# Forming delta*u*B of a selective scan on TensorE with a diagonal that GpSimd selects

## The chip, the cores and the metric

The kernel runs on one core of a Trainium2 chip. The metric is the device time of one execution in microseconds (us), lower is better. The engines of the core are TensorE (PE in the profile; the loading of its weights is PEld), VectorE (DVE), ScalarE (ACT), GpSimd (POOL) and SyncE (SP), which issues the DMAs. SBUF is the on-chip memory of 128 partitions, PSUM the memory that TensorE writes its results to.

## The reference

The model has four layers on 4 images of 64 x 64 pixels with 96 channels. Layers 0 and 1 are selective scans over the image in four directions; layers 2 and 3 are attention and a small network on tokens. The change touches only the scans. For each image, direction k and channel d (192 channels) the reference computes, over L = 4096 positions and 16 states n:

```
delta = softplus(dt_proj(dts) + bias)
dA = exp(delta * A[d, n])
h = dA * h + (delta * u) * B[n]        # one recurrence per channel and state
y = sum over n of h * C[n]             # B and C are projections of u, shared by all channels
result = y + D[d] * u                  # D is then summed over the four directions
```

B and C depend on position, state, direction and image, but not on the channel. The results of the four directions are added up.

## The kernel before, in words

Two images are scanned together, and there are two such pairs and two scan layers: four scans, each a `PairScan`. Partitions hold channels. An image has 192 channels, so a scan has three tiles of partitions: j = 0 holds 128 channels of the first image, j = 1 the same 128 of the second ("own" tiles), and j = 2 the remaining 64 channels of both (the "shared" tile). The sequence is cut into chunks of T = 1024 positions. A step is one (direction k, chunk ci, tile j), 4 x 4 x 3 = 48 steps a scan, 192 in all. A step goes through 16 states in 8 groups of NG = 2.

For each state DVE runs one hardware scan along the 1024 positions, `h = da * h + bp` (line 715). Its two inputs are da = exp(delta*A), from ScalarE, and delta*u*B. The latter is made in one of three ways, and a letter for each state in the strings OWN and SHARED (line 45) says which; `maker` looks it up:

- V: TensorE spreads the row of B over the partitions by a product with a selection matrix, `sel` (line 592), into the PSUM tile bp, and DVE multiplies it in place by du = delta*u (line 712).
- A: ScalarE scales the transposed du (`dut`, positions on partitions) by B, which is then a scalar per partition (`outer`, line 541; the tile x), and TensorE transposes the eight 128x128 blocks into bp (line 588).
- G: a DMA spreads the row of B over the partitions (tile bb, line 562), GpSimd multiplies it by du (tile dbu, line 575), and ScalarE writes the exponential into bp (line 585).

B in the transposed form is the tile bt, with positions on partitions, 8 blocks, and 32 columns (16 states of each image); it is the last entry of `projected`, and `dut` the last of `made`.

After the scan GpSimd copies the last value of each row for the next chunk (tile last, line 728) and multiplies h in place by C, which a DMA has spread over the partitions (tile cb, line 730). TensorE sums the 16 states: it transposes each h into the PSUM tile yp, where the passes accumulate (`onto_time`, line 617). The first term of yp is D*u in direction 0 (ScalarE scales u into the tile skip, line 636, and eight transposes add it), and in the other directions the sum so far, read back from memory (tile kept). ScalarE copies yp out (ysum, line 663).

All engines follow the program's order (`InOrder`), so the order of the main loop (line 680) is the order of each engine's queue. In the turn of group g it issues: the loads of bb for group g+2; the bp products of group g; the sum of group g-3 (LAG = 3; h has four buffers); what is made ahead for group g+1 (x, da, cb, dbu); the V products and the scans of group g; pieces of the next step's delta and du and of the next chunk's projection at fixed places (`drive`); and last, on GpSimd, the copy of last and the two C products of group g. bp has two buffers of PSUM, x has two, da four, cb three, dbu and bb one.

Every instruction inside the scans passes through the helper at line 71, so the profile puts them all on L71, and they are told apart by their tiles.

Of the kernel before, what the change touches and what calls it, by code (L numbers as in the profile page):

```python
# [16 lines left out]
F32 = mybir.dt.float32  # L17
BF16 = mybir.dt.bfloat16
# [3 lines left out]
ALU = mybir.AluOpType  # L22
# [4 lines left out]
HW = 64  # L27
# [4 lines left out]
D1 = DI - D0  # L32
NS = 16
R = 6
K = 4
NP = 32 * 3
# [3 lines left out]
T = 1024  # L40
NG = 2
LAG = 3


OWN, SHARED = "VAVAVAAGVAVAVAVA", "VGVAVAVGVAVGVAVV"
NT = L // 128
HID = 4 * C
EPS = 1e-5
# [7 lines left out]
class InOrder:  # L56


    def __init__(self, tc):
        for name in ("tensor", "vector", "scalar", "gpsimd"):  # L60
            setattr(self, name, InOrderEngine(tc, getattr(tc.nc, name)))
        self.sync = tc.nc.sync
# [22 lines left out]
class ScanLayer:  # L85


    def __init__(self, tc, pw, dram, x_src, w, n):
        nc = tc.nc

        self.last = n == 1
        self.x_src, self.w = x_src, w
        self.x_dst = dram.tile([NB * L, C] if self.last else [NB, C, L], F32, name=f"x{n + 1}")

        self.norms = [[], []]

        self.zg = [dram.tile([3, 128, L], F32, name=f"zg{n}{pr}") for pr in range(NB // 2)]
        self.y = [dram.tile([2, L, DI], F32, name=f"y{n}{pr}") for pr in range(NB // 2)]
        self.par = par = pw.tile([128, 2, P_ALL], F32, name=f"par{n}")
        nc.sync.dma_start(out=par, in_=w["par"].rearrange("s p c -> p s c"))  # L100

        self.amat = pw.tile([128, 2, K * NS], F32, name=f"amat{n}")
        nc.scalar.activation(self.amat, par[:, :, P_A : P_A + K * NS], AF.Exp)
        nc.vector.tensor_scalar(self.amat, self.amat, -1.0, None, ALU.mult)
        self.dsum = pw.tile([128, 2, 1], F32, name=f"dsum{n}")
        nc.vector.tensor_reduce(self.dsum, par[:, :, P_D : P_D + K], mybir.AxisListType.X, ALU.add)


class GroupNorm:
# [260 lines left out]
class PairScan:  # L370
# [5 lines left out]
    def __init__(self, tc, pk, pq, pd, cst, ident, u, layer, pr):  # L376
        self.tc, self.pk, self.pq, self.pd = tc, pk, pq, pd
        self.cst, self.ident, self.u = cst, ident, u
        self.par, self.amat, self.dsum = layer.par, layer.amat, layer.dsum
        self.w, self.y = layer.w, layer.y[pr]  # L380
        self.weights = {0: load_weights(tc.nc, pk, self.w, 0)}
        self.projected, self.made = [], []
# [103 lines left out]

    def scan(self, stage, nc):
        tc, ident, steps, projected, made = self.tc, self.ident, self.steps, self.projected, self.made
        amat, dsum, w, y, weights, chunk_of = self.amat, self.dsum, self.w, self.y, self.weights, self.chunk_of
        sel = self.cst["sel"]  # L490
        pk = self.pk
        p2 = stage.enter_context(tc.tile_pool(name="b_2", bufs=2))
# [20 lines left out]
                pieces[0] = next(pieces[1])  # L513

        groups = [(at, n) for at in range(len(steps)) for n in range(0, NS, NG)]
        of = (0, 128, 64)

        def maker(g, i):
            at, n0 = groups[g]
            return (SHARED if steps[at][2] == 2 else OWN)[n0 + i]  # L520
# [37 lines left out]
            return cb  # L558

        bbs = {}  # L560

        def start_bb(g):

            at, n0 = groups[g]
            for i in range(NG):
                if maker(g, i) == "G":
                    bbs[g, i] = p2.tile([128, 1, T], F32, name="bb", bufs=1)
                    spread(bbs[g, i], projected[at // 3][2], steps[at][2], 2 * NS + n0 + i)

        def start_dbu(g):  # L570
            out = {}
            for i in range(NG):
                if (g, i) in bbs:
                    out[i] = p2.tile([128, T], F32, name="dbu", bufs=1)
                    nc.gpsimd.tensor_tensor(out[i], made[groups[g][0]][1], bbs.pop((g, i))[:, 0], ALU.mult)
            return out

        def start_bp(g, i, xs):


            at, n0 = groups[g]
            _, _, j = steps[at]
            bp = pm.tile([128, T], F32, name="bp", bufs=2)
            if maker(g, i) == "G":
                exp_of(bp, g, i)
            elif maker(g, i) == "A":
                for t in range(T // 128):
                    nc.tensor.transpose(bp[:, 128 * t : 128 * t + 128], xs[i][:, t], ident)
            else:
                for hf in range(2):  # L590
                    cols = slice(512 * hf, 512 * hf + 512)
                    nc.tensor.matmul(
                        bp[:, cols],
                        sel[:, n0 + i, of[j] : of[j] + 128],
                        projected[at // 3][1][:, cols],
                        start=True,
                        stop=True,
                    )
            return bp
# [3 lines left out]
        def add_up(g, i, h):  # L603

            at, n0 = groups[g]
            n = n0 + i
            if n == 0:
                sums[at] = yp = pm.tile([128, T // 128, 128], F32, name="yp")
                if at in skips:
                    onto_time(yp, skips.pop(at), True, False)  # L610
                else:
                    before = kept.pop(at)
                    for t in range(0, T // 128, 4):
                        nc.tensor.matmul(yp[:, t : t + 4], ident, before[:, t : t + 4], start=True, stop=False)
            onto_time(sums[at], h[:, i], False, n == NS - 1)

        def onto_time(yp, v, first, final):

            for t in range(T // 128):
                nc.tensor.matmul(  # L620
                    yp[:, t],
                    v[:, 128 * t : 128 * t + 128],
                    ident,
                    start=first and t % 4 == 0,
                    stop=final and t % 4 == 3,
                    is_transpose=True,
                )

        skips = {}

        def start_skip(at):

            k, _, j = steps[at]
            if k == 0:
                skips[at] = p2.tile([128, T], F32, name="skip", bufs=1)
                nc.scalar.mul(
                    skips[at].rearrange("p (a b) -> p a b", b=HW), projected[at // 3][0][j], dsum[:, j // 2]
                )

        def places(at, tile_):  # L640
# [25 lines left out]

        for g in range(2):
            start_bb(g)
        ahead, cb_next, dbu_next = start_ahead(0), start_cb(0), start_dbu(0)
        hs = {}  # L670

        def sum_of(g):
# [7 lines left out]
        for g, (at, n0) in enumerate(groups):  # L680
# [9 lines left out]
                discretising = begun(begin_discretise(at + 1)) if at + 1 < len(steps) else []  # L690
            if n0 == 8 and at + 1 < len(steps):
                load_kept(at + 1)
            (da, xs), cb, dbu = ahead, cb_next, dbu_next
            if g + 2 < len(groups):
                start_bb(g + 2)

            bps = [start_bp(g, i, xs) for i in range(NG)]
            if g >= LAG:
                sum_of(g - LAG)
            if n0 == 0:  # L700
                start_skip(at)
            if n0 == NS - NG:
                drive(discretising, n0)
                drive(projecting, (j, n0))
            if g + 1 < len(groups):
                ahead, cb_next, dbu_next = start_ahead(g + 1), start_cb(g + 1), start_dbu(g + 1)

            hs[g] = h = p2.tile([128, NG, T], F32, name="h", bufs=LAG + 1)
            du = made[at][1]
# [230 lines left out]
def hybrid_kernel(ctx: ExitStack, tc: tile.TileContext, a):  # L940
# [14 lines left out]
    with ExitStack() as scans:  # L955
        pw = scans.enter_context(tc.tile_pool(name="s_w", bufs=1))
        pn = scans.enter_context(tc.tile_pool(name="s_n", bufs=1))
        units = []
        for n in range(2):
            layer = ScanLayer(tc, pw, dram, x, {k: a[f"l{n}_{k}"] for k in ("par", "wi", "wx", "wdt", "wo")}, n)  # L960
            units += [(layer, pr) for pr in range(NB // 2)]
            x = layer.x_dst
        units[0][0].after = units[2][0]
        with ExitStack() as scanning:
            pk = scanning.enter_context(tc.tile_pool(name="s_k", bufs=2))
            pu = scanning.enter_context(tc.tile_pool(name="s_u", bufs=1))
            pq = scanning.enter_context(tc.tile_pool(name="s_q", bufs=1))
            pd = scanning.enter_context(tc.tile_pool(name="s_d", bufs=2, space=DRAM))
            cst["sel"] = pu.tile([NP, NS, 256], BF16, name="sel")
            nc.sync.dma_start(out=cst["sel"], in_=a["c_sel"])  # L970
            cst["ident16"] = pu.tile([128, 128], BF16, name="ident16")
            nc.vector.tensor_copy(cst["ident16"], ident)
            u = [pu.tile([128, L], F32, name=f"u{j}") for j in range(3)]
            before = None
            for unit in units:
                scan = PairScan(tc, pk, pq, pd, cst, ident, u, *unit)
                between_scans(tc, cst, ident, half, pn, u, before, scan, unit)
                scan.run()
                before = unit
        token_layers(tc, cst, ident, half, x, before, a)  # L980


def constants():
# [2 lines left out]
    import numpy as np  # L986


    sel = np.zeros((3, 2, NS, NS, 2, 128), ml_dtypes.bfloat16)
    for n in range(NS):  # L990
        for i in range(2):
            sel[:, i, n, n, i] = 1
# [1 line left out]
    group = np.where(at[:, None] // 3 == at[None] // 3, np.float32(1) / np.float32(3), np.float32(0))  # L994
    heads = np.where(at[:, None] // 16 == at[None] // 16, np.float32(0.25), np.float32(0))
    return {
        "c_sel": sel.reshape(NP, NS, 256),
        "c_group": group.astype(np.float32),
        "c_heads": heads.astype(np.float32),
    }  # L1000
# [93 lines left out]
```

## Time and profile before

The profile page gives the profiled execution's own time only as its span.

| | |
|---|---|
| median of 3 runs | 10596.84 us (10596.55 to 10597.79) |
| span of the profiled execution | 10592.1 us |
| DVE busy | 9610.8 us (91%) |
| GpSimd busy | 9023.9 us (85%) |
| ScalarE busy | 8761.4 us (83%) |
| TensorE busy, weight loads | 8027.2 us (76%), 5946.6 us (56%) |
| mean granted TensorE clock | 0.885 |
| moved by DMA | 2120.41 MB, mean 200 GB/s |

How to read a row of the groups: line, engine, operation, output<-inputs, shape, xcount; then the busy time of the group in us and the mean duration of one instruction in ns; then the idle time of the engine just before these instructions, and what ended most of it. Busy time counts overlapping instructions once, so busy time divided by the count can be less than the mean. The two longest groups are GpSimd's product of h with C (3072 instructions, 7196.5 us) and DVE's scans (3072 in four groups).

### The profile page before, as it was taken

What the parts mean: (1) busy time and instruction counts of PE and PEld (TensorE: products, weight loads), DVE (VectorE), ACT (ScalarE), POOL (GpSimd) and SP (SyncE); (2) the same over time, 40 slices, a digit from 0 to 9 for tenths busy, and PEclk for the clock granted to TensorE, in tenths of its full rate; (3) what the DMA queues carried; (4) which work ended last, traced back from release to release, by engine and by line L of the source; (5) the groups of instructions that cost most, each with busy time, mean ns of one, the idle gap of its engine ahead of it and who ended that gap; (6) DMA issues with size and microseconds to landing.
All of it is one profiled execution on the core that took longest, in us unless ns stands there. A gap on an engine that the chain in (4) does not pass through costs nothing. (4 is left out here: it accounts for less than half of the span.)

```text
span 10592.1 us, 142441 instructions
## 1 busy us (share of the span) xinstructions
PE 8027.2 (76%) x47648; PEld 5946.6 (56%) x47648; DVE 9610.8 (91%) x6922; ACT 8761.4 (83%) x18779; POOL 9023.9 (85%) x5298
## 2 busy tenths in 40 slices
PE   7777777777777777777877777777877777777666
PEld 4555555554555555555555555555555565555554
DVE  8999999998999999998899999999799999999755
ACT  6888888885988888887788888888688888888666
POOL 3999999993999999997599999999399999999645
PEclk9888898989888898998888988898888989899877
DMA  5677777776677777777567777777667777777710
GB/s 155 208 212 216 220 220 218 219 218 164 205 212 212 218 220 218 217 220 210 158 206 213 219 220 220 223 213 216 162 207 212 216 213 225 221 217 213 195 32 25
DMA packets 905174, 2120.41 MB, mean 200 GB/s; under 512 B 330582, under 2 KB 640152, under 8 KB 706712
## 3 DMA queue, kind: packets, MB, share of 16 engines
q1 hardware_dynamic: 904440, 2111.30, 69.5%
q8 instruction: 378, 6.19, 0.3%
q14 instruction: 356, 2.92, 0.1%
HBM read 1949.56 MB, written 161.48 MB: 199 GB/s over the span
## 5 line engine op out<-in xcount | busy, mean ns | idle before, releaser
L71 POOL TENSOR_TENSOR h<-h,cb 128x1024 f32<-128x1024 f32 x3072 | 7196.5, 2367 | 226.4 <-issue 62.6
L71 DVE TENSOR_TENSOR_SCAN h<-da,last,bp 128x1024 f32<-128x1024 f32 x2064 | 4736.6, 2335 | 146.7 <-PE bp L71 22.8
L71 ACT ACTIVATE x<-dut,bt 128x128 f32<-128x128 f32 x12288 | 3495.9, 371 | 1.4 <-PE bp L71 1.1
L71 PE MATMUL yp<-ident,h 128*128 128x128 f32 x24576 | 3359.4, 297 | 10.5 <-POOL h L71 10.5
L71 PEld LDWEIGHTS yp<-ident,h 128*128 128x128 f32 x24576 | 3188.5, 157 | 126.6 <-issue 76.6
L71 ACT ACTIVATE da<-delta,amat 128x1024 f32<-128x1024 f32 x2752 | 3062.3, 1139 | 96.6 <-DVE h L71 95.8
L71 PE MATMUL bp<-ident,x 128*128 128x128 f32 x10240 | 1678.5, 316 | 1294.1 <-DVE h L71 956.8
L71 PEld LDWEIGHTS bp<-ident,x 128*128 128x128 f32 x10240 | 1361.3, 163 | 1854.8 <-ACT x L71 1017.4
L71 DVE TENSOR_TENSOR bp<-du,bp 128x1024 f32<-128x1024 f32 x1472 | 1780.5, 1214 | 259.8 <-PE bp L71 257.8
L71 DVE TENSOR_TENSOR_SCAN h<-da,bp 128x1024 f32<-128x1024 f32 x688 | 1537.7, 2275 | 49.9 <-ACT da L71 9.6
L71 PE MATMUL bp<-bparts,sel 96*128 96x512 bf16 x2944 | 920.5, 398 | 756.3 <-DVE h L71 740.4
L71 PEld LDWEIGHTS <-sel 96*128 96x128 bf16 x2944 | 226.8, 100 | 1550.2 <-DVE h L71 1037.8
L71 ACT ACTIVATE bp<-delta,amat 128x1024 f32<-128x1024 f32 x320 | 358.1, 1119 | 526.3 <-DVE h L71 524.6
L71 POOL TENSOR_TENSOR dbu<-du,bb 128x1024 f32<-128x1024 f32 x320 | 755.7, 2362 | 0.0
L71 DVE TENSOR_TENSOR_SCAN h<-bp,last,dbu 128x1024 f32<-128x1024 f32 x240 | 558.9, 2329 | 16.9 <-POOL dbu L71 15.9
L71 PE MATMUL xps<-u,wx 128*76 128x512 f32 x720 | 532.2, 824 | 0.0
L71 POOL COPY last<-h 128x2 f32<-128x2 f32 x1152 | 217.7, 189 | 357.2 <-DVE h L71 355.5
L81 POOL TENSOR_TENSOR ln_rs<-ln_ve,half 128x4 f32<-128x4 f32 x64 | 89.8, 1403 | 483.1 <-DVE ln_ve L79 405.9
L71 ACT ACT_TABLE_LOAD x380 | 487.5, 1283 | 15.9 <-PE bp L71 9.2
L71 POOL TENSOR_TENSOR du<-delta,u 128x1024 f32<-128x1024 f32 x188 | 496.8, 2642 | 0.0
L71 PE MATMUL dps<-cdt,wdt 12*128 12x512 f32 x752 | 433.6, 656 | 0.0
L71 ACT COPY ysum<-yp 128x1024 f32<-128x1024 f32 x192 | 194.5, 1013 | 287.1 <-PE yp L71 287.1
(159 smaller groups left out, 6312.6 us busy)
## 6 DMA issues: line engine op xcount, KB each, us to landing
cb<-crow SPq DMA_DIRECT2D x1024, 1024.0 KB
cb<-crow SPq DMA_DIRECT2D x1024, 512.0 KB
bb<-crow SPq DMA_DIRECT2D x384, 256.0 KB
bb<-crow SPq DMA_DIRECT2D x128, 512.0 KB
y<-ysum SPq DMA_DIRECT2D x192, 256.0 KB
kept<-y SPq DMA_DIRECT2D x160, 256.0 KB
y<-ysum SPq DMA_DIRECT2D x64, 512.0 KB
zt<-zg SPq DMA_DIRECT2D x64, 384.0 KB
```

Of the source, the lines that this page charges most:

```text
L71: return self.tc.keep_in_program_order(getattr(self.engine, op)(*args, **kwargs))
L81: nc.gpsimd.tensor_tensor(rs, ve, half, ALU.pow)
```

## The change

Part of the states of the own tiles are made in a fourth way, D. GpSimd forms, for each of the eight blocks of 128 positions, a 128x128 matrix with B of this state on its diagonal and zero elsewhere: an affine_select over the broadcast column of bt, 128x1024 elements in all (tile dg, one buffer). TensorE multiplies the transposed du block by it, which gives delta*u*B with channels on partitions, in bp. The OWN string goes from VAVAVAAGVAVAVAVA (7 V, 8 A, 1 G) to VDAAVDAAVDAAVAVA (5 V, 8 A, 3 D); SHARED stays. The selects for group g+1 are issued after the dbu products of group g+1, in the turn of group g.

D*u is added by TensorE: a diagonal matrix of D (tile skip of the layer, made once) is multiplied with u as the weights, into yp, in place of ScalarE's scaling and eight transposes.

The selection matrix has 128 columns a state in place of 256. For the shared tile they are used as they are; for an own tile one column is broadcast to 128 with a step of zero.

```diff
-OWN, SHARED = "VAVAVAAGVAVAVAVA", "VGVAVAVGVAVGVAVV"
+OWN, SHARED = "VDAAVDAAVDAAVAVA", "VGVAVAVGVAVGVAVV"
...
+        self.skip = pw.tile([128, 2, 128], F32, name=f"skip{n}")
+        for s in range(2):
+            nc.vector.tensor_scalar(self.skip[:, s], ident, self.dsum[:, s], None, ALU.mult)
...
-        of = (0, 128, 64)
...
+        zero = self.tc.nc.gpsimd.to_reg(0.0)
...
+        def start_diagonals(g):
+
+            at, n0 = groups[g]
+            j = steps[at][2]
+            out = {}
+            for i in range(NG):
+                if maker(g, i) == "D":
+                    out[i] = p2.tile([128, T // 128, 128], F32, name="dg", bufs=1)
+                    col = NS * j + n0 + i
+                    nc.gpsimd.affine_select(
+                        out=out[i],
+                        in_=projected[at // 3][4][:, :, col : col + 1].to_broadcast([128, T // 128, 128]),
+                        compare_op=ALU.is_equal,
+                        fill=zero,
+                        base=0,
+                        pattern=[[0, T // 128], [-1, 128]],
+                        channel_multiplier=1,
+                    )
+            return out
...
+            elif maker(g, i) == "D":
+                for t in range(T // 128):
+                    nc.tensor.matmul(
+                        bp[:, 128 * t : 128 * t + 128], made[at][2][:, t], dgs[i][:, t], start=True, stop=True
+                    )
             else:
+                if j == 2:
+                    chosen = sel[:, n0 + i]
+                else:
+                    chosen = sel[:, n0 + i, D1 * j : D1 * j + 1].to_broadcast([NP, 128])
                 for hf in range(2):
                     cols = slice(512 * hf, 512 * hf + 512)
                     nc.tensor.matmul(
                         bp[:, cols],
-                        sel[:, n0 + i, of[j] : of[j] + 128],
+                        chosen,
                         projected[at // 3][1][:, cols],
                         start=True,
                         stop=True,
...
-                if at in skips:
-                    onto_time(yp, skips.pop(at), True, False)
+                k, ci, j = steps[at]
+                if k == 0:
+                    for t in range(T // 128):
+                        there = T * ci + 128 * t
+                        nc.tensor.matmul(
+                            yp[:, t],
+                            self.u[j][:, there : there + 128],
+                            self.skip[:, j // 2],
+                            start=t % 4 == 0,
+                            stop=False,
+                        )
                 else:
...
-        def start_skip(at):
-
-            k, _, j = steps[at]
-            if k == 0:
-                skips[at] = p2.tile([128, T], F32, name="skip", bufs=1)
-                nc.scalar.mul(
-                    skips[at].rearrange("p (a b) -> p a b", b=HW), projected[at // 3][0][j], dsum[:, j // 2]
-                )
...
-            bps = [start_bp(g, i, xs) for i in range(NG)]
+            bps = [start_bp(g, i, xs, dgs) for i in range(NG)]
             if g >= LAG:
                 sum_of(g - LAG)
-            if n0 == 0:
-                start_skip(at)
...
             if g + 1 < len(groups):
                 ahead, cb_next, dbu_next = start_ahead(g + 1), start_cb(g + 1), start_dbu(g + 1)
+                dgs_next = start_diagonals(g + 1)
...
-            cst["sel"] = pu.tile([NP, NS, 256], BF16, name="sel")
+            cst["sel"] = pu.tile([NP, NS, 128], BF16, name="sel")
```

More of the change, by code (lines that the diff above doesn't have):

```diff
@@ L85, with __init__ @@
 class ScanLayer:
-    def __init__(self, tc, pw, dram, x_src, w, n):
+    def __init__(self, tc, pw, dram, ident, x_src, w, n):
         nc = tc.nc
@@ L378, in __init__ @@
         self.cst, self.ident, self.u = cst, ident, u
-        self.par, self.amat, self.dsum = layer.par, layer.amat, layer.dsum
+        self.par, self.amat, self.skip = layer.par, layer.amat, layer.skip
         self.w, self.y = layer.w, layer.y[pr]
@@ L488, in scan @@
         tc, ident, steps, projected, made = self.tc, self.ident, self.steps, self.projected, self.made
-        amat, dsum, w, y, weights, chunk_of = self.amat, self.dsum, self.w, self.y, self.weights, self.chunk_of
+        amat, w, y, weights, chunk_of = self.amat, self.w, self.y, self.weights, self.chunk_of
         sel = self.cst["sel"]
@@ L576, in start_dbu, with start_bp @@
             return out
-        def start_bp(g, i, xs):
+        def start_bp(g, i, xs, dgs):
             at, n0 = groups[g]
@@ L614, in add_up, with onto_time @@
                         nc.tensor.matmul(yp[:, t : t + 4], ident, before[:, t : t + 4], start=True, stop=False)
-            onto_time(sums[at], h[:, i], False, n == NS - 1)
-        def onto_time(yp, v, first, final):
+            onto_time(sums[at], h[:, i], n == NS - 1)
+        def onto_time(yp, v, final):
             for t in range(T // 128):
@@ L623, in onto_time @@
                     ident,
-                    start=first and t % 4 == 0,
+                    start=False,
                     stop=final and t % 4 == 3,
                     is_transpose=True,
-                )
-        skips = {}
-        def start_skip(at):
-            k, _, j = steps[at]
-            if k == 0:
-                skips[at] = p2.tile([128, T], F32, name="skip", bufs=1)
-                nc.scalar.mul(
-                    skips[at].rearrange("p (a b) -> p a b", b=HW), projected[at // 3][0][j], dsum[:, j // 2]
                 )
@@ L668, in scan @@
             start_bb(g)
-        ahead, cb_next, dbu_next = start_ahead(0), start_cb(0), start_dbu(0)
+        ahead, cb_next, dbu_next, dgs_next = start_ahead(0), start_cb(0), start_dbu(0), start_diagonals(0)
         hs = {}
@@ L692, in scan @@
                 load_kept(at + 1)
-            (da, xs), cb, dbu = ahead, cb_next, dbu_next
+            (da, xs), cb, dbu, dgs = ahead, cb_next, dbu_next, dgs_next
             if g + 2 < len(groups):
                 start_bb(g + 2)
-            bps = [start_bp(g, i, xs) for i in range(NG)]
+            bps = [start_bp(g, i, xs, dgs) for i in range(NG)]
             if g >= LAG:
                 sum_of(g - LAG)
-            if n0 == 0:
-                start_skip(at)
             if n0 == NS - NG:
@@ L959, in hybrid_kernel @@
         for n in range(2):
-            layer = ScanLayer(tc, pw, dram, x, {k: a[f"l{n}_{k}"] for k in ("par", "wi", "wx", "wdt", "wo")}, n)
+            layer = ScanLayer(tc, pw, dram, ident, x, {k: a[f"l{n}_{k}"] for k in ("par", "wi", "wx", "wdt", "wo")}, n)
             units += [(layer, pr) for pr in range(NB // 2)]
@@ L986, in constants @@
     import numpy as np
-    sel = np.zeros((3, 2, NS, NS, 2, 128), ml_dtypes.bfloat16)
+    sel = np.zeros((3, 2, NS, NS, 2, D1), ml_dtypes.bfloat16)
     for n in range(NS):
@@ L996, in constants @@
     return {
-        "c_sel": sel.reshape(NP, NS, 256),
+        "c_sel": sel.reshape(NP, NS, 128),
         "c_group": group.astype(np.float32),
```

## The prediction

> **What bounds the kernel now.** I read the page of the profile first (the busy row), then the windows view over a long stretch of one scan, then the groups, then the waits and the timeline. Busy row, from the page:
>
> ```profile
> PE 8027.2 (76%) x47648; PEld 5946.6 (56%) x47648; DVE 9610.8 (91%) x6922; ACT 8761.4 (83%) x18779; POOL 9023.9 (85%) x5298
> ```
>
> No engine is far behind another, so the share over the whole span settles nothing. The windows view of one stretch well inside the first scan (us from the start, length, busy us and instructions of PE, PEld, DVE, ACT, POOL, then clock and DMA):
>
> ```profile
> 300.00:2400.00 2100.00, 1601.70 (x9805) 1211.68 (x9804) 1991.38 (x1054) 1823.46 (x3910) 1976.73 (x1099) 0.90 0.75 217
> ```
>
> Inside a scan DVE is busy 1991.38/2100 = 94.8% and GpSimd 1976.73/2100 = 94.1%. These two bound the scans together; ScalarE has 86.8%, TensorE 76%. So time taken from DVE is worth only as much as GpSimd lets through. The groups give the prices; DVE and TensorE first, then GpSimd:
>
> ```profile
> L71 DVE TENSOR_TENSOR_SCAN h<-da,last,bp 128x1024 f32<-128x1024 f32 x2064 | 4736.6, 2335 | 146.7 <-PE bp L71 22.8
> L71 DVE TENSOR_TENSOR bp<-du,bp 128x1024 f32<-128x1024 f32 x1472 | 1780.5, 1214 | 259.8 <-PE bp L71 257.8
> L71 PE MATMUL bp<-ident,x 128*128 128x128 f32 x10240 | 1678.5, 316 | 1294.1 <-DVE h L71 956.8
> L71 PE MATMUL bp<-bparts,sel 96*128 96x512 bf16 x2944 | 920.5, 398 | 756.3 <-DVE h L71 740.4
> ```
>
> ```profile
> L71 POOL TENSOR_TENSOR h<-h,cb 128x1024 f32<-128x1024 f32 x3072 | 7196.5, 2367 | 226.4 <-issue 62.6 <-PE dps L71 34.5 <-PE yp L71 20.0
> L71 POOL TENSOR_TENSOR dbu<-du,bb 128x1024 f32<-128x1024 f32 x320 | 755.7, 2362 | 0.0
> L71 POOL COPY last<-h 128x2 f32<-128x2 f32 x1152 | 217.7, 189 | 357.2 <-DVE h L71 355.5 <-PE bp L71 1.0 <-PE xps L71 0.5
> masks.py:199 POOL TENSOR_SCALAR_AFFINE_SELECT ident<-ident 128x128 f32<-128x128 f32 x1 | 0.3, 294 | 0.0
> masks.py:197 POOL MEMSET ident<- 128x128 f32 x1 | 0.2, 205 | 0.3 <-POOLq L1084 0.3
> L1084 POOL MEMSET const-bfloat16-1.0<- 128x1 bf16 x1 | 0.1, 102 | 0.0
> ```
>
> The first two GpSimd rows show what it is full of: 3072 products with C. The fourth is the only run of the operation that the change adds, an eighth of the size. The waits (engine, line, for whom: total us, times, longest) show DVE and GpSimd taking turns, and what a G state costs ScalarE:
>
> ```profile
> ACT bp L71 <- DVE h L71: 524.6, 211, 6.1
> ...
> POOL last L71 <- DVE h L71: 355.5, 242, 31.6
> ...
> DVE bp L71 <- PE bp L71: 257.8, 325, 9.3
> ```
>
> The clock of the sum is the du product: GpSimd runs it once a step. In the timeline its starts go from 180.50 to 2377.48 us in the first scan, 46 steps, and over all four scans the step is 47.8 us: three steps (j = 0, 1, 2) take **143.5 us**. There are 64 such triples, 9184 us of the 10592.1 us of the profiled span; the other 1408 us (projections, token layers) are untouched.
>
> [...] Our row: 294 ns for 128 elements. The 128-element memset less the 1-element one is (205 - 102)/127 = 0.81 ns an element, and the select less the two-element copy (294 - 189)/126 = 0.83 ns[...]. [...] here the products' spans fit (2.34 us of busy time each against a span of 2.37). [...] no run here loads weights with step 0, the load from sel takes 100 ns.
>
> **The change, part by part.** Of the 192 steps 128 are own (j = 0, 1) and 64 shared (j = 2). The shared pattern stays. An own step goes from 7 V, 8 A, 1 G to 5 V, 8 A, 3 D.
>
> DVE, per own step: two products fewer, 2 x 1.21 = 2.43 us. The 16 scans stay. Per triple: 94.8% of 143.5 = 136.1 us now, less 4.85 = 131.2.
>
> GpSimd, per own step: one dbu fewer (2.36 us), three selects more. What a 128x1024 select costs is the open price, X. Low end: 102 + 1024 x 0.83 = 0.95 us. High end: eight times the 294 ns row, 2.35 us. [...] Fixed 189 ns and 0.83 ns an element: 1.04. The new pattern has eight rows of 128 and reads a broadcast column, which can only add, so I take X = 1.1. Per triple: 94.1% of 143.5 = 135.0, less 4.72, plus 6X: 130.3 + 6.6 = **136.9 us**, 1.9 more than now. A select stands in GpSimd's queue ahead of the copy of last and the two C products of the group before. The D passes on TensorE wait for it; queued behind them are the sixteen passes that sum an older group and the next group's bp, and DVE waits for those. The group ahead of a D is mostly a pair of A states, 4.6 us of DVE, against a C pair and a select, 4.68 + X on GpSimd: the D passes can start about X late, and DVE has its V product and a scan (1.21 + 2.3 us) to do first, so nothing is counted while X stays near 1. dg has one buffer, but the D states are two groups apart, so it is long free.
>
> TensorE, per own step: four bf16 passes of 313 ns (920.5/2944) go, 24 f32 passes come. At the transposes' 164 ns (1678.5/10240) that is 3.9 - 1.3 = +2.7 us, from 76% to about 82% of an own step. A true f32 product may be dearer; the convolution's 128x512 f32 row is busy 453 ns each (261.0/576), 113 per 128 columns[...]; the timeline has eight passes in 1.07 us at the full clock and 1.94 at the lower, and these are the two ends for a D state. Costed at nothing: TensorE's work hides under DVE's scans (4.58 us for two) and GpSimd's lag. Without that cover the 2.7 us would cost 128 x 2.7 = 346 us.
>
> ScalarE: exponentials are equally many (16 a step), the A states too. The G exponential into PSUM had to wait for DVE: 524.6/320 = 1.64 us each, 128 of them gone. The 48 skip scalings (1.14 us each, 54.5 us in all) go; TensorE adds D*u with eight passes in place of eight. ScalarE is not the bound: nothing counted. But A states now come in pairs: two times (8 x 0.304 + 1.11) = 7.1 us in one group, 2.2 in the next, where it was 4.7 in each.
>
> DMA: 128 loads of bb (512 KB) leave the sync queue, 67 of 2120 MB; GpSimd hardly waits for DMA, so nothing. Sel is loaded once at half size, four small DVE products are added at the start: under 3 us, nothing.
>
> The sum: DVE needs 131.2, GpSimd 136.9 of a triple, so GpSimd is left as the bound. How full can it get? 94.1% now, with DVE an equal partner; in windows of 100 us the fullest hold 97.5 to 97.7%. With DVE 5.7 us lighter than GpSimd I take 96.5%: 136.9/0.965 = 141.9, 1.6 less than 143.5; x 64 = -102 us. 10592 - 102 = 10490 of span; the median of the runs shown is 4.7 us over the span, so about **10495 us** (-1.0%).
>
> **The rivals.**
> B, the select is longer, and GpSimd makes it slower. Place: GpSimd's queue in own steps. Price: 6 us a triple per us of X. It decides from (143.5 x 0.965 - 130.3)/6 = 1.36 us on. At 1.75: 140.8/0.965 = 145.9, +154 us, 10751[...]; at 2.35 10990. For it: one short row of 294 ns is thin evidence, the other GpSimd operations cost 2.3 ns an element. Against: both slopes above.
> C, the paired A states. Around state 4 to 6 ScalarE has 7.1 + 2.2 and the softplus, its two table loads (2 x 1.28) and ysum, 4.9 us, together 14.2, while DVE is through the two groups in 5.8 + 4.6 = 10.4. Its lead of one group (about 5 us) covers the 3.8 missing. Without it DVE waits: 131.2/0.948 + 7.6 = 146.0, +160 us, 10757. Against: the G wait is gone.
> D, GpSimd goes on waiting as it does now, since it is DVE's bursts that starve it: 136.9/0.941 = 145.5, +128 us, 10725. For it: 355.5 us waiting for DVE. Against: DVE gets lighter.
> E, GpSimd's queue is hidden and DVE's saving comes through: 131.2/0.948 = 138.4, -326 us, 10271. Needs X near 0.9 and a full GpSimd.
>
> **How the numbers follow.** Likeliest case A 0.41, its own range 10400 (X 1.0, 97% full) to 10590 (X 1.34); B 0.28; C 0.13; D 0.11; E 0.07. A change of 0.2% (21 us) is about what can be told from none. Faster: 0.37 of A and E, 0.44. Within: 0.04 of A, 0.06 of B with X near 1.35, 0.01 each of C and D, 0.12. Slower: 0.22 + 0.12 + 0.10 = 0.44. The range 10380 to 10830 leaves out E and a little of A below (0.09), B above X = 1.95 and a tail of C above (0.10).
>
> **What would show it.** The select's row: 384 of them, mean near 1.1 us; over 1.36 speaks for B. The V row at 1216, dbu at 192. GpSimd near 96.5% in the same window, DVE near 92%. The waits: GpSimd for DVE's h well under 355.5 us and DVE for TensorE's bp not above 258 (A); the latter grown, with ScalarE's x behind it (C); GpSimd's wait unchanged (D). A load from a stride-0 column well over 100 ns, or D passes well over 164, would break the TensorE step.

## The result, and the profile after

The changed kernel takes 10639.6 us (median of 4 runs, 10636.06 to 10645.1) against 10596.7 us before: a ratio of 1.0044 (95% interval 1.0032 to 1.0057). It is slower by 0.44%, where 1.0% faster was forecast. The profiled execution has a span of 10642.9 us.

Busy row of the page, and the same stretch of the first scan in the windows view (busy us of PE, PEld, DVE, ACT, POOL):

```profile
PE 8483.3 (80%) x53664; PEld 6541.7 (61%) x53664; DVE 9331.1 (88%) x6670; ACT 8736.4 (82%) x18731; POOL 9135.3 (86%) x5554
```

```profile
300.00:2400.00 2100.00, 1703.12 (x11102) 1348.89 (x11101) 1908.98 (x985) 1807.88 (x3872) 1985.23 (x1151) 0.91 0.72 208
```

DVE went from 94.8% to 1908.98/2100 = 90.9%, as its lighter work says. GpSimd, which was to fill to 96.5%, is at 94.5%, hardly more than the 94.1% of before. Neither is full: both wait. The groups of the page that the prediction priced (a pass, here and below, is one matmul instruction of TensorE, one of the count behind the x):

```profile
L71 DVE TENSOR_TENSOR_SCAN h<-da,last,bp 128x1024 f32<-128x1024 f32 x2160 | 4955.2, 2335 | 396.5 <-PE bp L71 270.5
...
L71 DVE TENSOR_TENSOR bp<-du,bp 128x1024 f32<-128x1024 f32 x1216 | 1472.9, 1216 | 277.2 <-PE bp L71 272.0
...
L71 PE MATMUL bp<-dg,dut 128*128 128x128 f32 x6144 | 953.2, 320 | 420.6 <-POOL dg L71 248.5
...
L71 POOL TENSOR_SCALAR_AFFINE_SELECT dg<-bt 128x1024 f32<-128x1024 f32 x384 | 419.7, 1093 | 22.0 <-PE cps L192 20.8
```

The select costs 1.093 us, the 1.1 that was taken. But the D passes count 6144, not 384 x 8 = 3072: sixteen to a state. And the idle time before DVE's scans, put down to TensorE's bp, has become large. The waits view (who, at which tile, for whom: total us, times, longest), before:

```profile
PE bp L71 <- DVE h L71: 1697.1, 1188, 4.1
...
PE bp L71 <- ACT x L71: 312.0, 213, 3.1
...
DVE h L71 <- PE bp L71: 23.9, 24, 1.1
```

After:

```profile
PE bp L71 <- DVE h L71: 1197.5, 951, 3.5
...
PEld bp L71 <- POOL dg L71: 486.8, 279, 3.2
...
DVE h L71 <- PE bp L71: 380.9, 293, 2.5
...
POOL last L71 <- DVE h L71: 283.0, 283, 7.4
DVE bp L71 <- PE bp L71: 272.0, 354, 9.3
...
PE bp L71 <- ACT x L71: 170.7, 87, 2.6
```

Before, DVE waited for bp 257.8 us at V products and 23.9 at scans, 282 together; now 272.0 + 380.9 = 653. That is 371 us more of waiting against 1780.5 - 1472.9 = 308 us of products saved: 63 us lost on this account, and the span grew by 51. In the other direction TensorE, which waits for DVE's scan (h) to free a buffer of bp, does so for 1197.5 us in place of 1697.1: it is less far ahead of DVE than it was. So the loss sits in the step from DVE to TensorE and back. The timeline of one own step shows it, with lines for other engines' work left out (start us, us, engine; in brackets the idle time and what ended it). After:

```profile
1045.85 0.60 PE L71 MATMUL bp<-bparts,sel 96*128 96x512 bf16 x2
...
1046.29 1.09 POOL L71 TENSOR_SCALAR_AFFINE_SELECT dg<-bt 128x1024 f32<-128x1024 f32 x1
...
1047.44 2.05 PE L71 MATMUL bp<-dg,dut 128*128 128x128 f32 x16 [1.00 <-POOL dg L71]
...
1049.33 1.91 PE L71 MATMUL yp<-ident,h 128*128 128x128 f32 x16
...
1051.08 1.88 PE L71 MATMUL xps<-u,wx 128*76 128x512 f32 x2
...
1052.78 1.93 PE L71 MATMUL bp<-ident,x 128*128 128x128 f32 x16
...
1053.97 4.59 DVE L71 TENSOR_TENSOR_SCAN h<-da,last,bp 128x1024 f32<-128x1024 f32 x2 [1.54 <-PE bp L71]
```

TensorE has made the V product of the group and stands for 1.00 us in front of the D passes until the select ends. From there its queue runs without a gap: D, the sum of an older group, a projection, and only then the two A states of the next group. DVE has spent its cover by then and waits 1.54 us.

### The profile page after: what moved, and what is told of

It is laid out like the page before. It is cut to its first block, busy times and chain, and to the rows that moved or that the text cites. A ratio compares the mean times of both kernels' runs of the same rounds, so it can differ in the third digit from the quotient of the medians.

```text
span 10642.9 us, 154395 instructions
## 1 busy us (share of the span) xinstructions
PE 8483.3 (80%) x53664; PEld 6541.7 (61%) x53664; DVE 9331.1 (88%) x6670; ACT 8736.4 (82%) x18731; POOL 9135.3 (86%) x5554
## 5 line engine op out<-in xcount | busy, mean ns | idle before, releaser
L71 DVE TENSOR_TENSOR_SCAN h<-da,last,bp 128x1024 f32<-128x1024 f32 x2160 | 4955.2, 2335 | 396.5 <-PE bp L71 270.5
L71 ACT ACTIVATE da<-delta,amat 128x1024 f32<-128x1024 f32 x2880 | 3207.1, 1140 | 305.0 <-DVE h L71 300.9
L71 PE MATMUL bp<-ident,x 128*128 128x128 f32 x10240 | 1480.4, 296 | 520.9 <-DVE h L71 429.7
L71 DVE TENSOR_TENSOR bp<-du,bp 128x1024 f32<-128x1024 f32 x1216 | 1472.9, 1216 | 277.2 <-PE bp L71 272.0
L71 PE MATMUL bp<-bparts,sel 96*128 96x512 bf16 x2432 | 758.1, 398 | 717.3 <-DVE h L71 598.5
L71 PE MATMUL bp<-dg,dut 128*128 128x128 f32 x6144 | 953.2, 320 | 420.6 <-POOL dg L71 248.5
L71 PEld LDWEIGHTS bp<-dg,dut 128*128 128x128 f32 x6144 | 880.0, 228 | 603.3 <-POOL dg L71 486.8
L71 ACT ACTIVATE bp<-delta,amat 128x1024 f32<-128x1024 f32 x192 | 214.8, 1119 | 490.6 <-DVE h L71 488.8
L71 POOL COPY last<-h 128x2 f32<-128x2 f32 x1152 | 216.1, 188 | 310.1 <-DVE h L71 283.0
L71 POOL TENSOR_TENSOR dbu<-du,bb 128x1024 f32<-128x1024 f32 x192 | 452.5, 2357 | 0.0
L71 POOL TENSOR_SCALAR_AFFINE_SELECT dg<-bt 128x1024 f32<-128x1024 f32 x384 | 419.7, 1093 | 22.0 <-PE cps L192 20.8
```

The costliest lines, as they stand in the source:

```text
L71: return self.tc.keep_in_program_order(getattr(self.engine, op)(*args, **kwargs))
```

## The experiments

Three theories of the loss. **T1**: a D state costs TensorE twice what was counted. **T2**: the D passes wait for a select that GpSimd issues too late. **T3**: the paired A states (rival C). Every ratio is to the kernel before, timed together with the kernel named, with a 95% interval. All edits are against the changed kernel unless said.

**Without D states** (the parts of the change that remain: D*u on TensorE and the one-column selection).

```diff
-OWN, SHARED = "VDAAVDAAVDAAVAVA", "VGVAVAVGVAVGVAVV"
+OWN, SHARED = "VAVAVAAGVAVAVAVA", "VGVAVAVGVAVGVAVV"
```

> The change without its D states: the own pattern is that of before (7 V, 8 A, 1 G), D*u by TensorE and the one-column selection stay. All theories put the loss into the D states, so they expect no more than the skip scalings off ScalarE: 10,580 to 10,600 us, the same as before. If the load of weights with a step of zero, or the D*u passes, carried the loss, it would be near 10,640.

Measured 10563.4 us, 0.9968 (0.9956 to 0.9981). These parts gain 0.3% where nothing was counted. The D states, with the G and the two V that they replace, therefore cost 10640 - 10563 = 76 us on balance. What of the gain is the skip scaling and what the selection was not separated.

**A states unpaired.**

```diff
-OWN, SHARED = "VDAAVDAAVDAAVAVA", ...
+OWN, SHARED = "VAADVAADVAADVAVA", ...
```

> The same counts as after (5 V, 8 A, 3 D), but no two A states share a group: VA AD VA AD VA AD VA VA in place of VD AA VD AA VD AA VA VA; D stays second in its group. Theory T3 (the pairs of A leave DVE with 4.6 us a group and no V product to cover TensorE): DVE's waits for TensorE's bp fall from 653 us to near 300, time about 10,500. T1 (the sixteen passes of a D) and T2 (D waits for its select): the waits move but stay above 500 us, time 10,600 to 10,680.

Measured 10950.5 us, 1.0335 (1.0319 to 1.0350); DVE waits for bp 937 us. None of the theories expected this: the paired pattern is better than the mixed one, by 311 us. It is no clean test of T3, for the edit also puts each D behind an A where it stood behind a V. Rival C itself, ScalarE falling behind with x, is not seen in the changed kernel: TensorE's passes wait for x less than before (170.7 us, 312.0 before). Whether pairs cost something because they leave DVE without a V product stays open.

**Eight passes, the wait kept.**

```diff
-                    nc.tensor.matmul(
-                        bp[:, 128 * t : 128 * t + 128], made[at][2][:, t], dgs[i][:, t], start=True, stop=True
-                    )
+                    nc.tensor.transpose(bp[:, 128 * t : 128 * t + 128], dgs[i][:, t], ident)
```

> After, but a D state sends its diagonal through TensorE as eight transposes in place of the f32 product with du, so it has 8 passes instead of 16 and still waits for the select; du is left out of this state. T1: the D passes fall from 2.5 us of busy time to about 1.3 a state, DVE's waits for bp fall by 200 us or more, time 10,450 to 10,550. T2 and T3: within 30 us of 10,640.

Measured 10554.9 us, 0.9961 (0.9946 to 0.9976), 85 us under the changed kernel. The D row has 3072 passes and 508.1 us, 1.32 a state in place of 2.48:

```profile
L71 PE MATMUL bp<-ident,dg 128*128 128x128 f32 x3072 | 508.1, 319 | 428.6 <-POOL dg L71 296.6
```

DVE's waits for bp fell only from 653 to 593 us, where T1 had 200 us or more.

**Sixteen passes, no wait.**

```diff
-                        bp[:, 128 * t : 128 * t + 128], made[at][2][:, t], dgs[i][:, t], start=True, stop=True
+                        bp[:, 128 * t : 128 * t + 128], made[at][2][:, t], ident, start=True, stop=True
```

> After, but the D product takes the identity as its moving operand in place of the selected diagonal; the select is still made and nothing reads it, so a D has its 16 f32 passes and no wait for GpSimd. B is left out of these states. T2: the 487 us for which weight loads wait for dg go, DVE's waits for bp fall by 200 us or more, time 10,450 to 10,550. T1 and T3: within 30 us of 10,640, the waits for dg turn into waits for DVE's h.

Measured 10493.5 us, 0.9907 (0.9892 to 0.9922), 146 us under the changed kernel, with all its passes and all its selects. The wait is the larger of the two costs. DVE's waits for bp fell from 653 to 524 us, less than the 200 us of T2: more than half of what had been added stays without any wait for a select.

**The select one group earlier**, with a second buffer. This is the whole computation, and the cure that T2 asks for.

```diff
-                    out[i] = p2.tile([128, T // 128, 128], F32, name="dg", bufs=1)
+                    out[i] = p2.tile([128, T // 128, 128], F32, name="dg", bufs=2)
...
-                dgs_next = start_diagonals(g + 1)
+            if g + 2 < len(groups):
+                dgs_of[g + 2] = start_diagonals(g + 2)
```

> After, with each select issued one group earlier in GpSimd's queue (for group g+2 in the turn of g) and a second buffer for dg; the whole computation is kept. T2: the wait for dg goes as it did in nowait, GpSimd fills to about 96% of the scans, time 10,480 to 10,520. If nowait gained by something other than the lost wait, it stays near 10,640.

Measured 10497.1 us, 0.9907 (0.9892 to 0.9922). TensorE's wait for dg is 4 us; DVE's for bp 535. GpSimd is at 96.3% of the same stretch, from the windows view:

```profile
300.00:2400.00 2100.00, 1704.43 (x11281) 1346.11 (x11280) 1948.20 (x1006) 1836.06 (x3952) 2021.82 (x1168) 0.92 0.75 212
```

Its timeline at the place shown above:

```profile
1031.79 0.60 PE L71 MATMUL bp<-bparts,sel 96*128 96x512 bf16 x2
...
1032.23 1.95 PE L71 MATMUL bp<-dg,dut 128*128 128x128 f32 x16
...
1034.01 1.91 PE L71 MATMUL yp<-ident,h 128*128 128x128 f32 x16
...
1035.76 1.88 PE L71 MATMUL xps<-u,wx 128*76 128x512 f32 x2
...
1037.46 2.12 PE L71 MATMUL bp<-ident,x 128*128 128x128 f32 x16
...
1038.65 4.59 DVE L71 TENSOR_TENSOR_SCAN h<-da,last,bp 128x1024 f32<-128x1024 f32 x2 [0.28 <-ACT da L71]
```

The D passes follow the V passes at once. From the V passes to the next scan it is 6.86 us in place of 8.12.

**Is GpSimd the bound then?** Three kernels fill a table of passes and select, all without the wait and all without B in the D states. Eight passes: transposes of `made[at][2][:, t]` in place of the D product. No select: the affine_select and its tile left out.

> After, with D states as eight transposes of the transposed du itself: neither sixteen passes nor a wait for the select, which is still made and read by nothing. B is left out of these states. If GpSimd is the bound once the wait is gone (136.9 us of work in a triple), taking the passes away as well adds little: 10,440 to 10,490. If the two losses of 85 and 146 us add up: about 10,410.

> The kernel without the wait (identity as the moving operand, sixteen passes), and without the select too: 384 x 1.09 = 420 us less for GpSimd. B is left out of these states. If GpSimd is the bound there, as its 96.1% says, most of it shows until DVE or TensorE binds: 10,250 to 10,350. If TensorE's passes bind: 10,450 or more.

> The fourth cell of passes and select: D states as eight transposes and no select at all. B is left out of these states. With the select there, eight passes gained 15 us over sixteen (10,478 against 10,493), and without the select sixteen passes gave 10,503. If GpSimd's 420 us and TensorE's passes are two bounds at the same height, taking both away shows: 10,350 to 10,430. If what is left is DVE's own alternation with TensorE, within 30 us of 10,478.

| us (ratio) | sixteen passes | eight passes |
|---|---|---|
| select made | 10493.5 (0.9907) | 10478.4 (0.9892) |
| no select | 10502.9 (0.9912) | 10470.2 (0.9883) |

The intervals are about +-0.0015 each. The select with eight passes came out as expected if GpSimd is the bound (10,440 to 10,490), which alone would have misled; the kernels without a select did not. The select's 420 us of GpSimd's time are free here: without them the time does not fall beyond the intervals. The windows view of the kernel with sixteen passes and no select:

```profile
300.00:2400.00 2100.00, 1713.19 (x11269) 1354.80 (x11269) 1942.34 (x1003) 1830.93 (x3934) 1927.64 (x1076) 0.92 0.75 211
```

GpSimd is at 91.8%, the other engines where they were. What it no longer works it waits for DVE's h, 451.7 us where it was 157.2:

```profile
POOL last L71 <- DVE h L71: 451.7, 409, 30.4
```

GpSimd was not the bound, though it was 96% busy. The extra passes cost 15 to 33 us when nothing waits (the 15 lie within the intervals), 85 behind the wait.

**The number of D states, and their place**, with the early select.

```diff
-OWN, SHARED = "VDAAVDAAVDAAVAVA", ...
+OWN, SHARED = "VDAAVDAAVAVAVAVA", ...   # early2
+OWN, SHARED = "VDAAVDAAVDAAVDAA", ...   # early4
+OWN, SHARED = "VAVAVADAVAVAVAVA", ...   # earlyg
+OWN, SHARED = "VAADVAADVAADVAVA", ...   # earlyapart
```

> The early select with two D states in place of three (own pattern VD AA VD AA VA VA VA VA: 6 V, 8 A, 2 D); the whole computation is kept. GpSimd has 1.09 us less an own step and DVE 1.21 more than in early: if GpSimd alone binds, up to 128 x 1.09 = 140 us less than early, about 10,400; if the two engines bind together again, no gain: 10,480 to 10,530.

> The early select with four D states (VD AA four times: 4 V, 8 A, 4 D); the whole computation is kept. From two D to three the early kernel gained 54 us. If DVE's work is what counts, the fourth gains about as much, 10,430 to 10,470; GpSimd gets 1.09 us more an own step and is at 96% already, so if it binds: 10,500 to 10,640.

> The early select with one D in place of the G of before and all seven V kept (VA VA VA DA VA VA VA VA); the whole computation is kept. GpSimd gets 1.27 us less an own step than before, DVE as much as before. If GpSimd's share is what bounded before: 10,480 to 10,530. If DVE's work does: 10,550 to 10,600, like the kernel without D states (10,563).

> The early select with the pattern of apart (VA AD VA AD VA AD VA VA); the whole computation is kept. If apart's 10,951 came from the wait for the select alone, this is near early, 10,480 to 10,560. If it came from the cover (a D second in its group after an A has only one scan of 2.3 us ahead of it, after a V a product and a scan, 3.5 us), it stays above 10,650.

Two D: 10551.1 (0.9958, 0.9944 to 0.9973), neither of the two values expected: GpSimd has less to do than with three, and the kernel is slower. Three: 10497.1. Four: 10488.8 (0.9899, 0.9884 to 0.9914), between the two ranges expected, so the fourth gains nothing that can be told; GpSimd is 97.4% full there, which may be why, but this was not tried apart. One D for the G: 10637.5 (1.0039, 1.0024 to 1.0054), above both ranges expected and 74 us more than the kernel with the G, though GpSimd has less to do. So in this pattern taking the G away is a loss, where the prediction counted it as time won on GpSimd. Why stays unexplained; TensorE's passes wait for ScalarE's x 408 us there, against 323 without D. Unpaired: 10826.1 (1.0217, 1.0197 to 1.0236). The early select takes 124 us from the unpaired kernel, but its pattern alone still costs 329. That agrees with the cover: after a V a D has a product and a scan of DVE's ahead of it (3.5 us), after an A only a scan (2.3). This is argued, not isolated.

**The order of TensorE's queue.** The sum's sixteen passes stood between one group's second bp and the next group's first. Half of them are moved:

```diff
-            bps = [start_bp(g, i, xs, dgs) for i in range(NG)]
-            if g >= LAG:
-                sum_of(g - LAG)
+            bps = []
+            for i in range(NG):
+                bps.append(start_bp(g, i, xs, dgs))
+                if g >= LAG:
+                    add_up(g - LAG, i, hs[g - LAG])
+            hs.pop(g - LAG, None)
```

> The early select, and the sum of an older group is split in TensorE's queue: eight passes after the first bp of a group, eight after the second, in place of sixteen after the second. The whole computation is kept. If DVE's 535 us of waiting for bp come from the sixteen passes that stand ahead of the next group's bp: waits down to 350 us or less, time 10,330 to 10,430. If the waits come from the D and A passes themselves or from ScalarE's x: within 25 us of 10,497.

> The kernel without D states (7 V, 8 A, 1 G) with the same split of the sum. DVE waited 283 us for bp there, half of what it did in early, so at most half the gain: 10,500 to 10,565. If the split is worth the same with and without D states, it tells nothing of them.

> The changed kernel, select where the change put it, with the same split of the sum. The wait for dg holds the second bp of a group, so the sum's first half now passes ahead of it: 10,500 to 10,580 if the sum behind a waiting D is what passed the delay on to DVE; within 25 us of 10,640 if it is the late D itself.

Early: 10604.6 (1.0011, 1.0004 to 1.0018), 108 us worse. Without D states: 10414.9 (0.9832, 0.9816 to 0.9849), 149 better. The changed kernel: 10566.8 (0.9973, 0.9963 to 0.9983), 73 better. The expectations had early and the kernel without D the other way round. The gain of the changed kernel was expected if the sum behind a waiting D passes the delay on; since the split gains more where no D waits, it does not prove that. The waits of the split early kernel name a reason:

```profile
PE yp L71 <- ACT ysum L71: 332.4, 184, 2.4
DVE h L71 <- ACT x L71: 267.6, 85, 4.8
```

The first sum of a step has to wait until ScalarE has copied yp, 41.3 us in all in the early kernel. Moved ahead of a bp, it holds that bp, and DVE waits for x, 267.6 us where it was 1.0. That ScalarE's x waits for its buffer in between was not shown: x waits for bp 60.2 us here, 61.9 in the early kernel. So the last two kernels leave that one sum of each step unsplit:

```diff
+            split = g >= LAG and groups[g - LAG][1] > 0
...
+                if split:
+                    add_up(g - LAG, i, hs[g - LAG])
+            if split:
+                del hs[g - LAG]
+            elif g >= LAG:
+                sum_of(g - LAG)
```

> As the split early kernel, but the first sum of each step, which has to wait until ScalarE has copied yp, stays behind both bp products. The whole computation is kept. If that wait took over: TensorE's wait for ysum falls from 332 us to under 120, time 10,350 to 10,450. If the split itself harms the paired A states: about 10,600.

> The kernel without D states, split in the same way, the first sum of a step unsplit. The wait for ysum was 94 us there: 10,380 to 10,420, near the 10,415 of the full split. If D states are worth their passes once the order of TensorE's work is better, the early kernel is below this one; if not, above.

Early: 10407.4 us, 0.9824 (0.9810 to 0.9839), the fastest kernel here, 1.8% under before; the wait for yp fell to 100.3 us and DVE's wait for x to 1.7, as this reason says. Without D states: 10417.9, 0.9833 (0.9817 to 0.9850). The two intervals overlap: with a better order on TensorE, D states are worth about 0.1% (10.5 us), which these intervals cannot tell from nothing.

TensorE's mean granted clock moves with the order too: 0.889 to 0.907 from the kernel without D states to its split, 0.909 to 0.918 from early to the last split. How much of those gains is the clock's was not separated. It is not all: the first split of early has 0.911 and is 108 us slower than early at 0.909.

## Why the prediction was wrong

- **The select's price** (X = 1.1): right, 1.093. Rival B is out (its 1.75 us was the author's estimate); the broadcast column and the eight rows add 0.05 us at most to the 1.04 of its slopes.
- **"So nothing is counted while X stays near 1", of the D passes' wait for the select: this step failed.** It cost 146 us (the changed kernel against the kernel without the wait; 142 against the early select), about what lies between the forecast gain of 102 us and the loss of 43; that the two agree so closely is chance, since other terms were wrong as well. The select was no later than the prediction said (TensorE stands 1.00 us for it at the place shown, 248.5 us in all 384 states); it was the cover that it had wrong. The reasoning gave DVE's cover to the D passes alone. The same cover had to hold for all that stands behind them in TensorE's queue, the sum and the next group's two A states, and the prediction itself had named these.
- **TensorE, "24 f32 passes come"**: 48 come, and the passes of D*u are sixteen in place of eight (768 in all, 384 before). In the traces of before and after every f32 product that is no transpose has two passes (6144 for the 3072 of D, 768 for the 384 of D*u), an f32 transpose one (10240 for the 10240 of x). The trace of before showed it: 720 rows of xps for 360 products, and 576 rows of cps, from which the prediction took 453 ns a row, for 288. A D state is 2.48 us, not 1.31, so its eight products of 310 ns gave the sign that the prediction had named (well over 164). Costed at nothing, the extra passes cost 85 us behind the wait and 15 to 33 without.
- **"GpSimd is left as the bound", 6 us a triple per us of X: failed too.** Taking 420 us off it changed the time from 10493 to 10503. The forecast of 10495 is met almost to the us by the early select (10497), with the 96% that was taken, but not for the reason given: that is luck. What the runs point to as the limit is DVE and TensorE handing bp back and forth through two buffers: DVE lost 308 us of products and waits for bp 253 us more in the early kernel (535 against 282), 371 in the changed one, and moves in TensorE's queue alone change the time, from 149 us less to 108 us more. This is argued from waits: no run gave bp a third buffer.
- **Rival C**, the pairs of A states: not what happened. TensorE waits for ScalarE's x less than before (170.7 us against 312.0). Taking the pairs apart makes it slower, by 311 and 329 us, but moves the D as well.
- **Rival D** had the sign, and GpSimd at its old share (94.5%), but not the cause: its time, 10725, came from GpSimd's work, which was no bound where it was taken away, and GpSimd's wait for DVE's h was to stay at 355.5 us and is 283.0.
- **ScalarE's skip scalings and the selection, counted as nothing**: 0.3% faster together, with twice the passes for D*u that were counted. **Selection with a step of zero**: its loads take 100 ns as before (mean of 2432 loads from sel, shared tile included, and of 2944 before); right.

## What to carry to other kernels

When two engines are nearly full, test which of them is the bound before building on it: take work away from one of them in one run and see whether the time moves. An operand that another engine made just in time held here not only its own instruction but all that was queued behind it (TensorE stood 248.5 us for the selects, and issuing them a group earlier was worth 142 us), so a producer that is cheap should be issued a group earlier, where a buffer is free for it, before its price is judged. Count instructions from a row of the profile (its count for each product), not from the program.

## What the runs showed of the hardware

A 128x1024 f32 affine_select with a broadcast input took 1.09 us on GpSimd (mean of 384). An f32 product of 128x128 blocks took two passes: sixteen for 1024 columns, 2.0 us at a granted clock of 1.00 (at 1035.63 and 1047.44 us in the changed kernel) and 3.75 us at 1022.45 us, where it was 0.50 from 1022 to 1026; eight f32 transposes took 1.06 us at 1.00 (at 1039.24 us). Half of a group's sum moved ahead of another product in TensorE's queue was worth 1.4% in one kernel and cost 1.0% in another.
